# W2 in order of first appearance, W1 by id for 40 batches, row tables by three engines: an adapter layer with a language index

## The chip, the cores and the metric

The kernel runs on one core of a Trainium2 chip. The metric is the device time of one run in microseconds; the medians of several runs are compared. A core has five engines with queues of their own: TensorE (PE), VectorE (DVE), ScalarE (ACT), GpSimd (POOL) and SyncE (SP, here a queue of DMAs alone). Each works through its instructions in order and waits for the others by semaphores. The DMAs of all queues share 16 DMA engines.

## The reference

x holds 128 batches of 128 positions with 512 features, float32. Each batch has a language id (0 to 8 in the data, ten languages in the tables), and everything but x is looked up by it:

```
h       = relu(x @ W1[id] + b1[id])            # W1[id] 512x128
adapted = h @ W2[id] + b2[id]                  # W2[id] 128x512
y       = x + adapted
normed  = (y - mean(y)) * rsqrt(var(y) + 1e-5) # over the 512 features
out     = x + normed * gamma[id] + beta[id]
```

x and the output are 33.6 MB each; W1 and W2 are 2.6 MB each for all ten languages, 256 KB for one.

## The kernel before

One batch is one tile, 128 positions on the partitions. Loads of x come in groups of four batches (1 MB, four buffers), output leaves in pairs (512 KB, five buffers), both on SP's queue in program order. The order of each engine's instructions is written out by hand: `keep` ties an instruction to the one before it on its engine.

Per batch b the engines do this:

- PE: `transpose_x` (four products with the identity into the one buffer of pool `p_x`), `down` (W1, four chunks), `up` (W2, looked up in the table `w2` by a register holding the id).
- ACT: `copy_xT` (transposed x to SBUF), `relu`, `stage_w1` (copies W1 of this batch's id from a table in SBUF to `w1s`), `square` (sum of squares), and small work for mean and deviation.
- POOL: `add_b2` (r = x + b2[id], for most batches) and `add_beta` (o = x + beta[id]).
- DVE: `vector_b2` (the b2 add, for the batches that POOL leaves out), `residual` (adds r or x and sums), `scale` (minus mean, times gamma), `finish` (times rstd, plus o). `store` follows on SP.

The b2 row of a batch is added by one of three: POOL, DVE (`b2_by_vector`) or PE (`b2_by_matmul`, one more product that picks the row from `parts`).

The tables beta_b, gamma_b and b2_b hold each language's row on all 128 partitions (gamma's times -0.5). Before the loop, DVE splits the 30 rows into three bfloat16 parts, PE spreads each row with one product (`spread`, into the five buffers of pool `p_y` that `up` uses too), and DVE (17) and ACT (13) copy them out. These 30 turns stand between the first transposes, downs and relus.

W1 comes in two ways. Batches 0 to 8 (`FIRST`) read it from DRAM by their id, with the feature order "(p k)", so that x is transposed with a stride as well. From batch 9 `stage_w1` copies it from SBUF: up to batch 20 from `w1e` (same order, loaded in two DMAs), then from `w1` (four DMAs of 640 KB with rows of 512 bytes). W2 is loaded in id order, three languages and then seven.

In the loop, turn i transposes x of batch i, does down(i-1) and up(i-2), and the DVE work of batch b = i-3. A table indexed by a register is waited for as a whole, as far as the register's declared largest value reaches.

Of the kernel before, what the change touches and what calls it, by code (L numbers as in the profile page):

```python
# [16 lines left out]
P = 128  # L17
G = 4
EPS = 1e-5
FIRST = 9  # L20
EARLY = 21
LATE = 12
# [4 lines left out]
def cond_resid_kernel(ctx: ExitStack, tc: tile.TileContext, x, itok, W1, b1, W2, b2, gamma, beta, out):  # L27
# [31 lines left out]
    wp = ctx.enter_context(tc.tile_pool(name="wp", bufs=5))  # L59
# [18 lines left out]
    ids = const.tile([1, B], I32, name="ids")  # L78
# [3 lines left out]
    w1e = const.tile([P, L, KC, A], FP, name="w1e")  # L82
    w2 = const.tile([P, L * H], FP, name="w2")
    x_0 = xp.tile([P, G, H], FP, tag="x", name="x_0")
    xs[0] = x_0
# [5 lines left out]
    keep(nc.sync.dma_start(out=ids, in_=itok.rearrange("(o b) -> o b", o=1)))  # L91
    keep(nc.scalar.dma_start(out=rows[0:L, :], in_=beta))
    keep(nc.sync.dma_start(out=rows[L : 2 * L, :], in_=gamma))
    keep(nc.scalar.dma_start(out=rows[2 * L : 3 * L, :], in_=b2))
    load_part(0, 2)
# [4 lines left out]
    keep(nc.scalar.activation(warm, warm, AF.Abs_reciprocal_sqrt))  # L100
    def load_w1(k):
        keep(
            nc.sync.dma_start(out=w1[:, :, k, :], in_=W1[:, k * P : (k + 1) * P, :].rearrange("l p a -> p l a"))
        )

    ident = const.tile([P, P], FP, name="ident")
    make_identity(nc, ident)
    eps = const.tile([P, 1], FP, name="eps")
    nc.gpsimd.memset(eps, EPS)
    ones = const.tile([P, P], BF, name="ones")  # L110
    nc.gpsimd.memset(ones, 1.0)
# [3 lines left out]
    R = 3 * L  # L115
# [6 lines left out]
    keep(nc.vector.tensor_scalar(pick[:, L : 2 * L], pick[:, L : 2 * L], -0.5, None, ALU.mult))  # L122
# [4 lines left out]
    wrap = const.tile([1, B], I32, name="wrap")  # L127
    keep(nc.vector.tensor_scalar(wrap, ids, 0, L, ALU.is_lt, ALU.mult))
    lang = const.tile([1, B], I32, name="lang")
    keep(nc.vector.tensor_tensor(lang, ids, wrap, ALU.add))  # L130
    keep(nc.vector.tensor_scalar(lang, lang, 0, L - 1, ALU.max, ALU.min))

    def lid(b, engine):
        g = b // G
        if (g, engine) not in lids:
            loads, vals = nc.values_load_multi_w_load_instructions(  # L136
                lang[0:1, g * G : (g + 1) * G],
                engines=[engine],
                min_val=0,
                max_val=L - 1,  # L140
                skip_runtime_bounds_check_because="clamped on the chip to 0..L-1 above",
            )
            for ins in loads:
                keep(ins)
            lids[g, engine] = vals
        return lids[g, engine][b % G]

# [3 lines left out]
    def load_first(b):  # L151
        w1s[b] = wp.tile([P, KC, A], FP, tag="w1s", name=f"w1s_{b}")
        src = W1[bass.ds(lid(b, ET.SP), 1)].rearrange("o (p k) a -> p (o k a)", k=KC)
        keep(nc.sync.dma_start(out=w1s[b].rearrange("p k a -> p (k a)"), in_=src))

    def load_w2(lo, hi):
        dst = w2[:, lo * H : hi * H].rearrange("p (l h) -> p l h", l=hi - lo)
        keep(nc.sync.dma_start(out=dst, in_=W2[lo:hi].rearrange("l a h -> a l h")))

    def load_early(lo, hi):  # L160
        dst = w1e[:, lo:hi].rearrange("p l k a -> p l (k a)")
        keep(nc.sync.dma_start(out=dst, in_=W1[lo:hi].rearrange("l (p k) a -> p l (k a)", k=KC)))

    load_w2(0, 3)
    load_first(0)
    load_first(1)
    load_part(2, G)
    load_first(2)
    load_first(3)
    load_w2(3, L)  # L170
    xs[1] = xp.tile([P, G, H], FP, tag="x", name="x_1")
    for b in (G, G + 2):
        load_part(b, b + 2)
        load_first(b)
        load_first(b + 1)
    xs[2] = xp.tile([P, G, H], FP, tag="x", name="x_2")
    load_part(2 * G, 2 * G + 2)
    load_early(0, 5)
    load_first(2 * G)
    load_early(5, L)  # L180
    load_part(2 * G + 2, 3 * G)

    left = rp.tile([P, H], FP, tag="r", name="left")
    keep(nc.vector.tensor_copy(parts[0:R, :], rows[0:R, :]))
    keep(nc.vector.tensor_tensor(left[32 : 32 + R, :], rows[0:R, :], parts[0:R, :], ALU.subtract))
    keep(nc.vector.tensor_copy(parts[32 : 32 + R, :], left[32 : 32 + R, :]))
    keep(nc.vector.tensor_tensor(left[64 : 64 + R, :], left[32 : 32 + R, :], parts[32 : 32 + R, :], ALU.subtract))
    keep(nc.vector.tensor_copy(parts[64 : 64 + R, :], left[64 : 64 + R, :]))
# [7 lines left out]


    beta_b = const.tile([P, L * H], FP, name="beta_b")
    gamma_b = const.tile([P, L * H], FP, name="gamma_b")
    b2_b = const.tile([P, L * H], FP, name="b2_b")  # L200

    def spread(r, copier):
        t = (beta_b, gamma_b, b2_b)[r // L]
        row = p_y.tile([P, H], FP, tag="y", name=f"row_{r}")
        pick_r = pick[:, r : r + 1].to_broadcast([96, P])
        keep(nc.tensor.matmul(row, lhsT=pick_r, rhs=parts[:96, :], start=True, stop=True))
        dst = t[:, r % L * H : (r % L + 1) * H]
        if copier is nc.scalar:
            keep(nc.scalar.copy(dst, row))
        else:  # L210
            keep(nc.vector.tensor_copy(dst, row))  # L211
# [5 lines left out]
    def b2_by_matmul(b):  # L217
        return b in (5, B - 1)

    def b2_by_vector(b):  # L220
        return b < 4 or 8 <= b < B - 8 and (b % 4 == 1 if b < 24 else b % 16 in (1, 6, 11) or b % 32 == 30)

    def stage_w1(b):
        w1s[b] = wp.tile([P, KC, A], FP, tag="w1s", name=f"w1s_{b}")
        src = (w1e if b < EARLY else w1).rearrange("p l k a -> p (l k a)")[:, bass.ds(lid(b, ET.Activation) * (KC * A), KC * A)]
        keep(nc.scalar.copy(w1s[b].rearrange("p k a -> p (k a)"), src))  # L226

    def transpose_x(b):
        pxs[b] = p_x.tile([P, KC, P], FP, tag="xT", name=f"pxT_{b}")
        for k in range(KC):  # L230
            if b < EARLY:
# [36 lines left out]
    def up(b):  # L268
        v = lid(b, ET.PE)
        ys[b] = p_y.tile([P, H], FP, tag="y", name=f"py_{b}")  # L270
        m = b2_by_matmul(b)
        if m:
            pick_b = pick[:, bass.ds(v + 2 * L, 1)].to_broadcast([96, P])
# [216 lines left out]
    spin(9, H)  # L490
    spin(1, H // 2)

    def spread_turn(lo, hi):
        for r in range(lo, hi):
            spread(r, nc.scalar if r % 7 in (1, 3, 5) else nc.vector)
# [4 lines left out]

    x_turn(0)
    transpose_b1()
    spread_turn(0, 4)
    x_turn(1)
    spread_turn(4, 11)
    down(0)
    relu(0)
    spread_turn(11, 15)
    down(1)
    relu(1)  # L510
    x_turn(2)
    spread_turn(15, 19)
    x_turn(3)
    down(2)
    relu(2)
    spread_turn(19, 24)
    down(3)
    relu(3)
    spread_turn(24, R)
    up(0)  # L520
    up(1)

    for i in range(3, B + U):
# [3 lines left out]
        if i == 5:  # L527
            load_x(3)
        if i in (8, 10, 12, 14):
            load_w1((i - 8) // 2)  # L530
        if i == 4:
            up(2)
        if i == 5:
            up(3)
        if i > 3 and on(i):
            transpose_x(i)
# [3 lines left out]
        if i > 4 and on(i - 1):  # L540
            down(i - 1)
        if i > 3 and on(i):
            copy_xT(i)
# [3 lines left out]
        if i > 4 and on(i - 1):  # L547
            relu(i - 1)
        if i + 1 >= LATE and on(i + 1):
            stage_w1(i + 1)  # L550
        if i > 5 and on(i - U):
# [41 lines left out]
        if FIRST <= i + 1 < LATE:  # L593
            stage_w1(i + 1)
# [41 lines left out]
```

## Time and profile before

| what | value |
|---|---|
| median of 3 runs | 308.49 us (308.26 to 308.88) |
| span of the profiled execution | 306.5 us |
| median less span | 2.0 us |
| PE, DVE, ACT, POOL busy | 294.6, 295.9, 282.3, 283.9 us |
| DMA moved | 77.85 MB, 254 GB/s on average |
| granted TensorE clock | 0.989 |

The profile is one execution; its own time is the span, from the first to the last instruction, and the sums of the prediction are made against it. A line of the timeline has start and duration in us, the engine, the source line, the operation with the tile written and read, the shape and the count, and in brackets the idle time before it with what ended it. A line of the waits has who waited, for whom, and total us, times and longest us. A duration of POOL overlaps that of its neighbour, so that its pitch is read from starts. PEld and PEldq are PE's weight loads and their queue; a q behind an engine's name is its instruction queue.

### The profile page before, as it was taken

To read this page: it belongs to the slowest core of one execution; us is meant where nothing else is said; L and a number is where in the kernel's file an instruction comes from. 1 tells how busy PE (TensorE), PEld (TensorE's weight loads), DVE (VectorE), ACT (ScalarE), POOL (GpSimd) and SP (SyncE) were. 2 spreads that over 40 slices of the span, in tenths; PEclk is the share of its full clock that TensorE was granted. 3 is DMA by queue.
4 is the path that set the end of the run, shared out by engine and by line. 5 is a ranking of instruction groups with operands and counts; after the bars stand their busy time and mean duration, and the time that the engine had idled before them with its cause. 6 is when DMAs were issued, how large, how long until landed. Compare 5 with 4: busy or idle time off the path is not lost. (4 is left out here: it accounts for less than half of the span.)

```text
span 306.5 us, 6981 instructions
## 1 busy us (share of the span) xinstructions
PE 294.6 (96%) x1835; PEld 220.0 (72%) x1835; DVE 295.9 (97%) x771; ACT 282.3 (92%) x777; POOL 283.9 (93%) x238
## 2 busy tenths in 40 slices
PE   8999999999999999999999999999999999999960
PEld 3748787777777777777777777777777777777730
DVE  6889999999999999999999999999999999999985
ACT  3858999999999999999999999999999999999981
POOL 1349899999999999999999999999999999999994
PEclk9999999999999999999999999999999999999995
DMA  6999999976678766766777666767776666773324
GB/s 231 379 390 388 373 371 354 387 231 240 221 255 276 250 202 241 226 257 219 259 276 243 213 209 238 265 224 260 275 238 206 226 231 242 246 266 137 135 109 171
DMA packets 43769, 77.85 MB, mean 254 GB/s; under 512 B 1961, under 2 KB 7348, under 8 KB 43730
## 3 DMA queue, kind: packets, MB, share of 16 engines
q1 hardware_dynamic: 43382, 76.84, 72.1%
q10 hardware_dynamic: 348, 0.57, 0.5%
q8 instruction: 15, 0.25, 0.3%
q14 instruction: 24, 0.20, 0.2%
HBM read 43.85 MB, written 33.55 MB: 253 GB/s over the span
## 5 line engine op out<-in xcount | busy, mean ns | idle before, releaser
L252 POOL TENSOR_TENSOR o<-x,beta_b 128x512 f32<-128x512 f32 x128 | 173.9, 1395 | 10.2 <-DVE beta_b L211 9.5
L245 POOL TENSOR_TENSOR r<-x,b_b 128x512 f32<-128x512 f32 x97 | 135.7, 1399 | 7.3 <-DVE b_b L211 6.2
L258 PE MATMUL ph<-xT,w1s 128*128 128x128 f32 x1024 | 135.4, 275 | 0.0
L275 PE MATMUL py<-w,hT 128*128 x256 | 131.2, 595 | 0.5 <-DVE b_b L211 0.5
L258 PEld LDWEIGHTS ph<-xT,w1s 128*128 128x128 f32 x1024 | 124.9, 192 | 1.0 <-ACT hT L266 0.5
L235 PEld LDWEIGHTS pxT<-ident,x 128*128 128x128 f32 x512 | 66.6, 151 | 65.3 <-issue 49.2
L358 DVE SCALAR_TENSOR_TENSOR py<-py,nmean,gamma_b 128x512 f32<-128x512 f32 x126 | 95.0, 754 | 0.9 <-ACT sq L399 0.8
L367 DVE SCALAR_TENSOR_TENSOR o<-py,rstd,o 128x512 f32<-128x512 f32 x122 | 91.2, 748 | 0.0
L315 ACT ACTIVATE sq<-py,sum 128x512 f32<-128x512 f32 x124 | 85.9, 693 | 2.8 <-DVE py L292 2.5
L235 PE MATMUL pxT<-ident,x 128*128 128x128 f32 x512 | 78.2, 276 | 0.0
L239 ACT COPY xT<-pxT 128x512 f32<-128x512 f32 x128 | 74.7, 584 | 3.5 <-PE pxT L235 3.5
L292 DVE SCALAR_TENSOR_TENSOR py<-py,r 128x512 f32<-128x512 f32 x97 | 67.0, 691 | 0.2
L226 ACT COPY w1s<-w 128x512 f32 x107 | 65.5, 612 | 0.0
L266 ACT ACTIVATE hT<-ph,b1T 128x128 f32<-128x128 f32 x128 | 46.9, 366 | 7.9 <-PE ph L258 2.6
L275 PEld LDWEIGHTS py<-w,hT 128*128 128x128 f32 x256 | 39.1, 192 | 2.9 <-issue 1.0
L315 ACT ACTIVATION_READ_ACCUMULATOR sq<-py,sum 128x1 f32 x124 | 25.0, 202 | 0.0
L292 DVE SCALAR_TENSOR_TENSOR py<-py,x 128x512 f32<-128x512 f32 x31 | 21.7, 699 | 0.4
L285 DVE TENSOR_TENSOR py<-py,b_b 128x512 f32<-128x512 f32 x29 | 20.2, 695 | 0.7 <-PE py L275 0.6
L325 ACT ACTIVATE root<-ssq,eps 128x2 f32<-128x2 f32 x62 | 16.4, 265 | 0.0
L292 DVE DVE_READ_ACCUMULATOR py<-py,r 128x1 f32 x97 | 13.7, 141 | 0.0
L306 ACT ACTIVATE nmean<-sum 128x2 f32<-128x2 f32 x62 | 12.3, 198 | 0.0
L329 DVE SCALAR_TENSOR_TENSOR part<-ssq,root 128x2 f32<-128x2 f32 x62 | 9.3, 151 | 0.2 <-ACT root L325 0.2
(55 smaller groups left out, 90.4 us busy)
## 6 DMA issues: line engine op xcount, KB each, us to landing
out_dram<-o SPq DMA_DIRECT2D x61, 512.0 KB, 3.4
x<-in_x_dram SPq DMA_DIRECT2D x29, 1024.0 KB, 6.2
x<-in_x_dram SPq DMA_DIRECT2D x6, 512.0 KB, 8.8
w1e<-in_L_cond_W_dram SPq DMA_DIRECT2D x2, 1280.0 KB, 12.3
w<-in_L_cond_W_dram SPq DMA_DIRECT2D x4, 640.0 KB, 8.1
w1s<-in_L_cond_W_dram SPq DMA_DIRECT2D x9, 256.0 KB, 8.4
w<-in_L_cond_W_dram SPq DMA_DIRECT2D x1, 1792.0 KB, 10.3
w<-in_L_cond_W_dram SPq DMA_DIRECT2D x1, 768.0 KB, 5.4
```

The source lines that it names most:

```text
L226: keep(nc.scalar.copy(w1s[b].rearrange("p k a -> p (k a)"), src))
L235: keep(nc.tensor.transpose(pxs[b][:, k, :], cols, ident))
L239: keep(nc.scalar.copy(xT[b], pxs.pop(b)))
L245: keep(nc.gpsimd.tensor_tensor(rs[b], xb(b), b2_b[:, bass.ds(v * H, H)], ALU.add))
L252: keep(nc.gpsimd.tensor_tensor(os[g][:, j, :], xb(b), beta_b[:, bass.ds(v * H, H)], ALU.add))
L258: nc.tensor.matmul(phs[b], lhsT=w1s[b][:, k, :], rhs=xT[b][:, k, :], start=(k == 0), stop=(k == KC - 1))
L266: keep(nc.scalar.activation(hT[b], phs.pop(b), AF.Relu, bias=b1T[:, bass.ds(lid(b, ET.Activation), 1)]))
L275: keep(nc.tensor.matmul(ys[b], lhsT=hT[b], rhs=w2[:, bass.ds(v * H, H)], start=not m, stop=True))
L292: nc.vector.scalar_tensor_tensor(ys[b], ys[b], 1.0, r, ALU.mult, ALU.add, accum_out=col(sums, b))
L315: nc.scalar.activation(sq, ys[b], AF.Square, bias=col(sums, b), scale=-float(H), accum_out=col(ssqs, b))
L358: nc.vector.scalar_tensor_tensor(ys[b], ys[b], col(nmeans, b), gamma_b[:, bass.ds(v * H, H)], ALU.add, ALU.mult)
L367: nc.vector.scalar_tensor_tensor(o, ys.pop(b), rstds[g][:, j : j + 1], o, ALU.mult, ALU.add)
```

## The change

- The ids are read onto ten partitions. VectorE finds the place of each language's first batch, one product with PE and a comparison give its rank, and two more products give `slots`: which language has each rank, and the rank of each batch's language. `load_slot(j)` loads the W2 of the language of rank j into slot j; `up(b)` takes the slot, and for b under 10 the slot is declared to be at most b, so that up(b) waits for slots 0 to b alone.
- W1 is read by id for batches 0 to 39 (`BY_ID`) into seven buffers (`RING`, before five); the table `w1e` and its 12 staged batches are gone, and `stage_w1` begins at batch 40. `ahead` strings W1, W2 and x loads together; the four `w1` loads stand at turns 16, 21, 26 and 31, before at 8, 10, 12 and 14.
- beta's rows: loaded at partitions 0, 32, 64 and 96, spread by ten VectorE shuffles of 128x512. b2's: loaded as one flat row on partition 0, spread by two GpSimd broadcasts of 2,560 columns each. gamma's ten rows stay with PE and ACT, five before up(0) and five in turns 3 to 5. The bfloat16 parts are taken by reading the upper halves of the float32 words.
- Batches 0 to 3 get b2 from PE (before from VectorE), batch 5 from GpSimd (before from PE).
- Six warming products stand at the start, before nine and a half; batches 0 to 2 (before 0 to 3) are transposed before the loop.

```diff
-FIRST = 9
-EARLY = 21
-LATE = 12
+BY_ID = 40
+RING = 7
...
+    lang = const.tile([L, B + 1], I32, name="lang")
+    keep(nc.sync.dma_start(out=lang[:, 0:B], in_=itok.rearrange("(o b) -> o b", o=1).to_broadcast([L, B])))
+    beta_rows = rp.tile([P, H], FP, tag="r", name="beta_rows")
+    nc.gpsimd.memset(beta_rows, 0.0)
+    for q in range(2):
+        keep(nc.scalar.dma_start(out=beta_rows[32 * q : 32 * q + L, :], in_=beta))
+    load_part(0, 1)
+    keep(nc.scalar.dma_start(out=rows[0:L, :], in_=gamma))
+    for q in range(2, 4):
+        keep(nc.scalar.dma_start(out=beta_rows[32 * q : 32 * q + L, :], in_=beta))
+    load_part(1, 2)
+    keep(nc.scalar.dma_start(out=rows[L : 2 * L, :], in_=b2))
+    load_part(2, 4)
+    keep(nc.scalar.dma_start(out=b2_b[0:1, :], in_=b2.rearrange("(o l) h -> o (l h)", o=1)))
     keep(nc.scalar.dma_start(out=b1r, in_=b1))
...
+    keep(nc.vector.scalar_tensor_tensor(seen, lang, own, weight, ALU.is_equal, ALU.mult))
+    keep(nc.vector.tensor_reduce(first, seen, mybir.AxisListType.X, ALU.max))
...
+    def rank_languages():
+        order = p_s.tile([P, H], FP, tag="s", name="order")
+        keep(nc.tensor.matmul(order[:L, 0:L], lhsT=first.to_broadcast([L, L]), rhs=ident[:L, :L], start=True, stop=True))
+        keep(nc.vector.tensor_tensor(rows[32 : 32 + R, :], rows[0:R, :], upper(rows, 0), ALU.subtract))
+        keep(nc.vector.tensor_scalar(above, order[:L, 0:L], first, None, ALU.is_gt, ALU.add, accum_out=rank))
+        keep(nc.vector.tensor_scalar(own_of, lang[:, 0:B], own, None, ALU.is_equal))
+        keep(nc.vector.tensor_scalar(place, count[:, 0:L], rank, None, ALU.is_equal))
+        keep(nc.vector.tensor_tensor(parts[64 : 64 + R, :], rows[32 : 32 + R, :], upper(rows, 32), ALU.subtract))
+        keep(nc.scalar.copy(parts[0:R, :], upper(rows, 0)))
+        keep(nc.scalar.copy(parts[32 : 32 + R, :], upper(rows, 32)))
+        return order
+
+    def place_languages(order):
+        keep(nc.tensor.matmul(order[:1, L : 2 * L], lhsT=own, rhs=place, start=True, stop=True))
+        keep(nc.tensor.matmul(order[:1, 2 * L : 2 * L + B], lhsT=rank, rhs=own_of, start=True, stop=True))
+        keep(nc.vector.tensor_copy(slots, order[:1, L : 2 * L + B]))
...
-    def load_first(b):
+    def load_by_id(b):
...
-    def load_w2(lo, hi):
-    def load_early(lo, hi):
+    def load_slot(j):
+        if j == 0:
+            v = lid(0, ET.SP)
+        else:
+            if not perm:
+                perm.extend(values(slots[0:1, 1:L], ET.SP, L - 1))
+            v = perm[j - 1]
+        src = W2[bass.ds(v, 1)].rearrange("o a h -> a (o h)")
+        keep(nc.sync.dma_start(out=w2[:, j * H : (j + 1) * H], in_=src))
...
-    def spread(r, copier):
+    def spread_gamma(lo, hi):
+        for r in range(lo, hi):
+            row = p_y.tile([P, H], FP, tag="y", name=f"row_{r}")
+            pick_r = pick[:, r : r + 1].to_broadcast([96, P])
+            keep(nc.tensor.matmul(row, lhsT=pick_r, rhs=parts[:96, :], start=True, stop=True))
+            keep(nc.scalar.copy(gamma_b[:, r * H : (r + 1) * H], row))
+
+    def spread_beta(lo, hi):
+        for r in range(lo, hi):
+            keep(nc.vector.stream_shuffle(beta_b[:, r * H : (r + 1) * H], beta_rows, [r] * 32))
+
+    def spread_b2(lo, hi):
+        cols = slice(lo * H, hi * H)
+        keep(nc.gpsimd.partition_broadcast(b2_b[:, cols], b2_b[0:1, cols]))
...
     def b2_by_matmul(b):
-        return b in (5, B - 1)
+        return b < 4 or b == B - 1
...
     def up(b):
-        v = lid(b, ET.PE)
+        v = slot(b)
...
-    spin(9, H)
-    spin(1, H // 2)
+    spin(6, H)
+    order = rank_languages()
...
+    def ahead(n):
+        if n == 3:
+            load_slot(1)
+            load_part(4, 6)
+        elif n == 5:
+            load_part(6, 8)
+        elif n == 7:
+            load_part(8, 10)
+        elif n == 9:
+            load_part(10, 12)
+        load_by_id(n)
+        if 3 < n < L + 2:
+            load_slot(n - 2)
+
+    spread_b2(0, L // 2)
+    spread_b2(L // 2, L)
     x_turn(0)
     transpose_b1()
-    spread_turn(0, 4)
+    place_languages(order)
     x_turn(1)
-    spread_turn(4, 11)
+    spread_gamma(0, 2)
+    spread_beta(0, 3)
     down(0)
     relu(0)
+    spread_gamma(2, 4)
+    spread_beta(3, 6)
+    x_turn(2)
+    for n in range(3, RING + 1):
+        ahead(n)
     down(1)
     relu(1)
...
+    spread_gamma(4, 5)
+    spread_beta(6, 10)
     up(0)
...
-        if i in (8, 10, 12, 14):
-            load_w1((i - 8) // 2)
+        if i in (16, 21, 26, 31):
+            load_w1((i - 16) // 5)
...
+        if i + RING - 2 < BY_ID:
+            ahead(i + RING - 2)
+        if i < 6:
+            spread_gamma(2 * i - 1, min(2 * i + 1, L))
...
-        if i + 1 >= LATE and on(i + 1):
+        if BY_ID <= i + 1 and on(i + 1):
             stage_w1(i + 1)
```

## The prediction

> **What bounds the kernel now.** I read the page's busy shares first, then the waits, then the timelines of PE and POOL from end to end, and last the DMA by stretches.
>
> ```profile
> PE 294.6 (96%) x1835; PEld 220.0 (72%) x1835; DVE 295.9 (97%) x771; ACT 282.3 (92%) x777; POOL 283.9 (93%) x238
> ```
>
> Four engines are over 90% busy, so no share names the bound; the waits do. All long ones of the engines lie in the first 20 us:
>
> ```profile
> POOL o L252 <- DVE beta_b L211: 9.5, 1, 9.5
> POOL r L245 <- DVE b_b L211: 6.2, 1, 6.2
> POOL r L245 <- DMA x<-in_x_dram: 1.1, 1, 1.1
> ```
>
> POOL waits for the row tables beta_b and b2_b, then once for x, and never again. Its timeline (start, us, line, count):
>
> ```profile
> 10.98 2.50 POOL L252 TENSOR_TENSOR o<-x,beta_b 128x512 f32<-128x512 f32 x2 [9.53 <-DVE beta_b L211]
> 19.67 1.27 POOL L245 TENSOR_TENSOR r<-x,b_b 128x512 f32<-128x512 f32 x1 [6.19 <-DVE b_b L211]
> ...
> 296.34 1.45 POOL L415 TENSOR_TENSOR n<-n,gamma_b 128x512 f32<-128x512 f32 x1
> ```
>
> From 19.67 to 296.34 it does 126 of the 128 beta adds and 97 b2 adds: (276.67 - 1.14 of wait) / 223 = 1.235 us each. PE:
>
> ```profile
> 18.94 2.81 PE L275 MATMUL py<-w,hT 128*128 x6 [0.46 <-DVE b_b L211]
> ...
> 26.92 0.63 PE L235 MATMUL pxT<-ident,x 128*128 128x128 f32 x4
> 29.36 0.63 PE L235 MATMUL pxT<-ident,x 128*128 128x128 f32 x4
> 31.58 0.63 PE L235 MATMUL pxT<-ident,x 128*128 128x128 f32 x4
> ...
> 290.88 0.60 PE L235 MATMUL pxT<-ident,x 128*128 128x128 f32 x4
> ```
>
> Batch 9 is transposed at 31.58, batch 127 at 290.88: 2.197 us a batch for 118 batches, back to back (transposes 0.43, down 0.90, up 0.86). So PE and POOL both run without a gap from about 20 us to about 296, and then comes a tail of 10 us. The end is the start of the steady stretch plus a fixed amount of work, on either engine: only the first 20 us can shorten. DVE has room once it starts: in its timeline two batches without a b2 add take 4.07 us (149.83 to 153.90).
>
> ```profile
> 28.00:32.00 4.00, 4.00 (x25) 3.02 (x25) 4.00 (x12) 3.12 (x10) 4.00 (x4) 1.00 1.05 382
> 44.00:48.00 4.00, 4.00 (x26) 3.05 (x26) 4.00 (x11) 3.86 (x13) 4.00 (x4) 1.00 1.08 344
> 52.00:56.00 4.00, 4.00 (x26) 3.06 (x26) 4.00 (x12) 3.86 (x12) 3.57 (x3) 1.00 1.08 397
> ```
>
> The last two columns are DMA share and GB/s: full at 380 to 390 until 62 us, and 344 to 373 (mean 360) from 36 to 52, where w1's 512-byte rows are read. After 64 us it is 240.
>
> **Start, part by part.** Only sums that reach POOL or PE count.
>
> POOL's first work grows by the memset of beta_rows. Memsets of 128x1 and 128x128 take 98 and 204 ns, so 128x512 is about 0.5 us. `ident`, with an iota ahead of it, comes 0.65 later. DVE's clamp of the ids moves from 2.80 to 3.45, and so does the first W1 load of SP, from 3.55 to 4.2. ACT's DMA queue holds seven small loads for two and waits for that memset: issues of about 0.33 us from 1.4 on, b2's rows at 3.35, the flat b2 row at 3.7, then the table load (1.28), ACT free at 5.95. Small loads landed 1.7 us after issue (b2's rows: 1.41, used at 3.1), so rows are there at 5.05 and the flat row at 5.7 (20 KB on one partition).
>
> DVE, in order: subtraction 5.05 (0.68), three small ops of 0.22 for rank and place, subtraction 0.68, b1T, slots: the ranking ends at 7.45. The two extra PE products (0.23 each, as b1p) lie in that time. Against before, DVE loses 17 copies (0.64 each, 10.9 us) and three casts, and gets ten shuffles. The trace has no shuffle: the cheapest row of 512 columns is the cast (0.42), the dearest DVE row 0.76; I take 0.62, the pitch of copies and residuals that also move one word per column. beta_b is complete at 7.45 + 6.2 = 13.65 (11.7 to 15.1).
>
> ACT and PE: two part copies (0.4) to 6.75, xT of batch 0 to 7.4, which frees the one transpose buffer. Then they alternate: row product 0.23, row copy 0.54, down 0.9, relu 0.35, up with its bias product 1.1. In turn: down(0) ends 9.2, relu(0) 9.9, xT(2) 11.55, up(0) starts 11.3 (18.94 before). Turns 3 to 5 still carry five gamma copies on ACT ahead of xT, 3.2 us a turn: batches 4, 5 and 6 are transposed at 15.65, 18.85 and 21.5, batch 7 at 23.8, where before has 26.92, and batch 9 at 28.2 for 31.58. So PE gains 3.4 us. The 20 row products that go (4.6 us) are more than that, since ACT is the slower partner here. The single register loads of the first ten batches (0.33 each on PE's queue) are hidden under 2.2 us of queued products a batch.
>
> POOL: the b2 broadcast writes 5,120 columns. Bounds from rows: the memset's slope (0.83 ns a column) gives 4.3 us, the two-input add (2.41) 12.35; nearest is the affine select, one tensor in and one out, (292 - 98)/127 = 1.5 ns, 7.8 us. From 5.7 it ends at 13.5 (10.0 to 18.05). The built program also selects another POOL code library ahead of the broadcasts and the first one again behind them. Before has one such selection ahead of the affine select, which started at 1.16 with POOL's memset just over: zero cost there. I take zero, and keep the dear end as a rival. So POOL's first add waits for both tables and starts at 14.2, half a microsecond after beta_b. From there it has 226 adds (128 and 98: batch 5 comes to POOL, batches 0 to 3 were never on it): 226 x 1.235 = 279.1, and L415 starts at 293.3 for 296.34. POOL gains 3.0 us. Break-even is a first add at 17.2.
>
> DVE: four b2 adds less (0.7 each), start 13.65 for 20.13: it gains more than both and follows. ACT loses the w1s copies of batches 9 to 39 (31 x 0.51), off the path: it has had slack.
>
> **DMA.** W1 by id for 40 batches is 10.5 MB, with w2 and w1 15.7 against 10.2 before: 5.5 MB more in the full stretch. A unit of 256 KB takes 0.68 us at 388 GB/s. A by-id batch moves three (x, W1, output): 2.03 us, under PE's 2.20. SP's queue now holds W2's slot 1, and all behind it, until the ranking is read, about 8.3. Down to batch 12's W1 there are 39 units: landed at 3.0 + 0.8 lost in that wait + 39 x 0.68 = 30.3, wanted at 28.2 + 3 x 2.2 + 2.65 = 37.4: 7 us in hand. 28 batches add 4.8; the four w1 loads (2.62 MB at 360 and the slowing of what runs beside them) take 8. So 3.8 us stay at batch 40: hidden, narrowly. SP issues W1 in line behind output stores that wait for DVE, so a load goes out some 11 to 14 us ahead of its product; loads of this kind took
>
> ```profile
> DMA to landing us min/median/max: 4.5/8.4/10.4
> ```
>
> from issue to landing. That is the cover, and 1 to 3 us of PE time are lost where it fails.
>
> **Sum.** PE -3.4, POOL -3.0; the later decides: -3.0. The span 306.5 becomes 303.5; the runs' median lies 2.0 above the span, so 305.5.
>
> **Rivals.**
> 1. *The library change is a code load* (ends slower). POOL stands at it twice, at 2.45 and behind the broadcasts, and every add queues behind. If each takes what the shortest W1 load took to land, 4.5 us, the first add is at 2.45 + 4.5 + 7.8 + 4.5 = 19.3, 2.1 us past break-even: 310.6; at the median 8.4 it is 27.1 and 318. It decides from 3.5 us each. For it: two changes that before has not. Against: the one selection there cost nothing, though that may be since the library was already in. I take 312 for it.
>
> The Trainium skill (GPSIMD Engine Reference, section 2.1, Instruction dispatch) says that the first call into a freshly loaded kernel pays a code load of about 6 us that no instruction in the profile shows. By it the sum would be a first add at 22.3 us and a run of 313.5, an estimate from that page; no run here shows it so far, and the zero gap ahead of the affine select speaks against it only if that library too was fresh.
>
> 2. *DMA runs dry between batches 16 and 40.* If the mixed rate stays at 360 rather than 388, a by-id batch takes 2.18 us, nothing is regained, and the w1 loads leave the queue about 1 us short, with the late issue 1 to 3: 306.5 to 308.5. For it: 344 in one stretch; against: 397 with stores running.
> 3. *The broadcast costs what an add costs a column*, 12.35 us: first add 18.05, 0.85 later than break-even: 309.3. For it: POOL's only wide operation here has that price; against: it reads two tensors.
>
> **Numbers.** Forecast 0.50 (own range 304.2 to 306.3, from beta_b at 13 to 15), rival 1 0.27, rival 2 0.15, rival 3 0.08. The range 304.2 to 312.3 leaves out the dear half of rival 1 and a little below. Less than 0.2% (0.6 us) can't be told from no change. Faster: 0.50 and most of rival 2, 0.62. Same 0.05, from rivals 2 and 3. Slower 0.33.
>
> **What would show it.** Right: POOL's first add near 14 and no POOL wait later, up(0) near 11.3, batch 9 transposed near 28, batch 127 near 287.5, DMA at 380 to 100 us with no PE wait for w1s. Wrong: a gap on POOL of several us on either side of the broadcasts (rival 1), PE waiting for DMA w1s around 50 to 95 us (rival 2), or shuffles over 0.97 us each, which would put beta_b past 17.2.

## The result and the profile after

The changed kernel takes 315.81 us (median, 315.61 to 317.11) where the kernel before takes 308.48 (308.26 to 308.88): ratio 1.0245, 95% interval 1.0226 to 1.0265. It is slower by 7.3 us, and the prediction's range, 304.2 to 312.3, does not hold it. The profiled span is 313.9 us for 306.5.

The page's line of busy shares, changed kernel:

```profile
PE 293.9 (94%) x1820; PEld 219.5 (70%) x1820; DVE 290.9 (93%) x774; ACT 269.1 (86%) x745; POOL 291.4 (93%) x246
```

PE's and DVE's shares fell a little and ACT's by six points; no new engine is full. Of the waits that are new (us in total, times, longest), four bear on what follows:

```profile
POOL o L303 <- DVE py L343: 10.2, 1, 10.2
POOL b_b L262 <- DVE parts L177: 7.4, 1, 7.4
...
PE b1p L246 <- DMA b1r<-in_L_cond_b_dram: 4.8, 1, 4.8
...
PE pxT L286 <- DMA x<-in_x_dram: 1.7, 3, 0.7
```

POOL stands 7.4 us ahead of b2's broadcasts and 10.2 behind them. POOL's timeline (start, us, line, idle before) shows what that does:

```profile
10.10 5.48 POOL L262 PARTITION_BROADCAST b_b<-b_b  x2 [7.41 <-DVE parts L177]
25.75 2.50 POOL L303 TENSOR_TENSOR o<-x,beta_b 128x512 f32<-128x512 f32 x2 [10.18 <-DVE py L343]
...
304.38 1.27 POOL L466 TENSOR_TENSOR n<-n,gamma_b 128x512 f32<-128x512 f32 x1
```

The releasers named are not the cause. The broadcasts end at 15.58, the last of beta's shuffles at 17.92 in VectorE's timeline, and the first add comes 7.8 us after that. The timeline shows nothing in between. Asked for by source line, the profile does: POOL's queue holds an instruction that changes POOL's code library (count, duration in ns, first and last start in us), here in the kernel before and then twice in the changed kernel:

```profile
masks.py:199 POOLq MODIFY_POOL_CONFIG  x2: 11/11/11, 1.1 to 1.1; - x2
L262 POOLq MODIFY_POOL_CONFIG  x2: 1/1/1, 2.7 to 2.7; - x2
L303 POOLq MODIFY_POOL_CONFIG  x2: 127/127/127, 15.5 to 15.5; - x2
```

The one in the kernel before cost nothing (its affine select starts at 1.16), nor did a first one at 1.7 in the changed kernel. Behind the two shown for the changed kernel, POOL stands until 10.10 and until 25.75. From 25.75 the 226 adds run without a gap, 1.233 us each, and the first multiply of the tail stands at 304.38 for 296.34: 8.0 later.

PE's timeline, batches 0, 1 and 9 and the last:

```profile
4.68 0.75 PE L286 MATMUL pxT<-ident,x 128*128 128x128 f32 x4
10.26 0.27 PE L246 MATMUL b1p<-ident,b1r 10*128 10x10 f32 x1 [4.83 <-DMA b1r<-in_L_cond_b_dram]
...
12.80 1.80 PE L309 MATMUL ph<-xT,w1s 128*128 128x128 f32 x8
...
16.68 1.02 PE L326 MATMUL py<-w,hT 128*128 128x512 f32 x2
...
34.32 0.63 PE L286 MATMUL pxT<-ident,x 128*128 128x128 f32 x4
...
297.73 0.60 PE L286 MATMUL pxT<-ident,x 128*128 128x128 f32 x4
```

PE does nothing between 5.4 and 10.3 us, since the transpose of b1 waits for b1's small load. Batch 9 is transposed at 34.32 for 31.58, batch 127 at 297.73 for 290.88. So PE is 2.7 us late after the start and 6.9 at the end. Of the other 4.1, 3.8 are lost between batches 10 and 40, which take 70.0 us for 66.2.

DMA by stretches (the last two columns are its share and GB/s), kernel before:

```profile
0.00:16.00 16.00, 14.76 (x75) 8.89 (x76) 11.57 (x26) 9.32 (x18) 3.37 (x10) 1.00 0.84 309
16.00:64.00 48.00, 47.55 (x292) 36.08 (x291) 46.94 (x118) 42.69 (x119) 42.54 (x35) 1.00 1.05 375
64.00:104.00 40.00, 40.00 (x255) 30.21 (x255) 39.88 (x105) 39.22 (x110) 40.00 (x33) 1.00 0.69 228
```

and the changed kernel:

```profile
0.00:16.00 16.00, 9.35 (x43) 6.12 (x44) 9.01 (x34) 6.12 (x12) 7.33 (x15) 0.79 0.49 164
16.00:64.00 48.00, 46.73 (x282) 34.69 (x281) 39.71 (x105) 36.02 (x101) 38.25 (x32) 1.00 1.04 381
64.00:104.00 40.00, 38.62 (x239) 29.41 (x238) 38.14 (x99) 29.82 (x85) 40.00 (x34) 1.00 1.06 392
```

Multiplied out, DMA has moved 4.9 MB at 16 us before and 2.6 after: 2.3 MB behind, 5.9 us at 390 GB/s. From there it is full until 104 us, where before it was full only until 62.

The issues of ScalarE's and SyncE's queues show where the first 16 us went:

```profile
4.20 0.29 ACTq L105 DMA_DIRECT2D rows<-in_L_cond_b_dram  x1
4.53 0.26 ACTq L107 DMA_DIRECT2D b_b<-in_L_cond_b_dram  x1
6.92 0.29 ACTq L108 DMA_DIRECT2D b1r<-in_L_cond_b_dram  x1
7.23 1.28 ACT L112 ACT_TABLE_LOAD   x1 [7.23 <-DMA rows<-in_L_cond_b_dram]
```

```profile
6.68 0.85 SPq L223 DMA_DIRECT2D w1s<-in_L_cond_W_dram  x2
13.51 0.33 SPq L235 DMA_DIRECT2D w<-in_L_cond_W_dram  x1
```

In the built program the loads of both queues use eight completion semaphores in turn, and a load is not issued before the one eight earlier has landed. So b1's load waits from 4.8 to 6.92, the table load behind it to 7.23, the ranking ends at 11.42 with PE's b1 wait inside it, and SyncE, which reads the ranked slots ahead of everything else, issues nothing for 6 us. The last 1.9 of these are the read itself, nine values at once (duration in ns, start in us):

```profile
L188 SPq TENSOR_LOAD <-slots x1: 1875/1875/1875, 11.4 to 11.4; - x1
```

SyncE's reads of a single id in the kernel before took 304 to 491 ns.

Two bounds, then, are each some 7 us late by themselves: POOL (first add 25.75) and PE (batch 127), whose loss behind the start falls into the stretch in which DMA is now full. The experiments take them apart.

### The profile page after: what moved, and what is told of

Its sections match the earlier page's. It is cut to its first block, busy times and chain, and to the rows that moved or that the text cites. A ratio compares the mean times of both kernels' runs of the same rounds, so it can differ in the third digit from the quotient of the medians.

```text
span 313.9 us, 7122 instructions
## 1 busy us (share of the span) xinstructions
PE 293.9 (94%) x1820; PEld 219.5 (70%) x1820; DVE 290.9 (93%) x774; ACT 269.1 (86%) x745; POOL 291.4 (93%) x246
## 4 chain that ended last, share of the span: by engine, by line
PE 41%; POOL 30%; DMA 13%; issue 10%; POOLq 2%; DVE 1%; ACT 1%; ACTq 1%; SPq 0%; DVEq 0%
POOL o L303 18%; PE ph L309 16%; PE py L326 14%; POOL r L296 11%; PE pxT L286 9%; DMA x<-in_x_dram 7%; DMA w1s<-in_L_cond_W_dram 2%; DMA out_dram<-o 2%; DMA beta_rows<-in_L_cond_beta_dram 1%; POOLq L188 1%; DMA b1r<-in_L_cond_b_dram 1%; POOL n L466 1%; PE row L253 1%; POOLq L296 1%; POOL o L468 1%
## 5 line engine op out<-in xcount | busy, mean ns | idle before, releaser
L303 POOL TENSOR_TENSOR o<-x,beta_b 128x512 f32<-128x512 f32 x128 | 161.4, 1269 | 10.2 <-DVE py L343 10.2
L326 PE MATMUL py<-w,hT 128*128 (+1 forms) x256 | 131.3, 594 | 0.0
L296 POOL TENSOR_TENSOR r<-x,b_b 128x512 f32<-128x512 f32 x98 | 124.1, 1266 | 0.0
L286 PEld LDWEIGHTS pxT<-ident,x 128*128 128x128 f32 x512 | 68.1, 161 | 71.2 <-issue 44.5
L286 PE MATMUL pxT<-ident,x 128*128 128x128 f32 x512 | 79.8, 279 | 2.7 <-DMA x<-in_x_dram 1.7
L343 DVE SCALAR_TENSOR_TENSOR py<-py,r 128x512 f32<-128x512 f32 x98 | 67.7, 691 | 2.1 <-PE py L326 0.8
L277 ACT COPY w1s<-w 128x512 f32 x88 | 53.9, 613 | 0.0
L336 DVE TENSOR_TENSOR py<-py,b_b 128x512 f32<-128x512 f32 x25 | 17.3, 692 | 0.9 <-PE py L326 0.7
L262 POOL PARTITION_BROADCAST b_b<-b_b x2 | 5.5, 2800 | 7.4 <-DVE parts L177 7.4
```

The lines of the kernel that those rows point to most:

```text
L286: keep(nc.tensor.transpose(pxs[b][:, k, :], cols, ident))
L296: keep(nc.gpsimd.tensor_tensor(rs[b], xb(b), b2_b[:, bass.ds(v * H, H)], ALU.add))
L303: keep(nc.gpsimd.tensor_tensor(os[g][:, j, :], xb(b), beta_b[:, bass.ds(v * H, H)], ALU.add))
L326: keep(nc.tensor.matmul(ys[b], lhsT=hT[b], rhs=w2[:, bass.ds(v * H, H)], start=not m, stop=True))
L343: nc.vector.scalar_tensor_tensor(ys[b], ys[b], 1.0, r, ALU.mult, ALU.add, accum_out=col(sums, b))
```

## Experiments

Times are medians; the kernel before, run beside them, is 308.46 to 308.77. "First add" is POOL's first beta add, "b10", "b40" and so on the start of that batch's transposes, read off PE's timeline (before: 33.8 and 100.0).

### Each bound taken away: a1, c1, c2

a1 puts a memset where the two broadcasts stood, so POOL changes no library for them (b2's table is zeros).

```diff
-        keep(nc.gpsimd.partition_broadcast(b2_b[:, cols], b2_b[0:1, cols]))
+        keep(nc.gpsimd.memset(b2_b[:, cols], 0.0))
```

> The changed kernel with a GpSimd memset of b2's table in place of the two broadcasts, so b2 is left out for the batches that read the table. No second code library is needed. Theory S (the change of library delays POOL's adds): POOL's first add starts within 0.3 us of the last shuffle, near 18.0 instead of 25.75, and the time falls from 315.8 to about 311, where the late PE start (batch 9 transposed at 34.3, 2.7 us later than before) becomes the bound. Rival (POOL waited for DVE or a load): the first add stays near 25 and the time at 315 to 316.

315.47 us (1.0225, 1.0187 to 1.0263). POOL's timeline of a1:

```profile
7.54 4.49 POOL L262 MEMSET b_b<- 128x2560 f32 x2 [5.15 <-DMA b_b<-in_L_cond_b_dram]
17.54 2.50 POOL L303 TENSOR_TENSOR o<-x,beta_b 128x512 f32<-128x512 f32 x2 [5.51 <-DVE beta_b L258]
```

The first add comes 8.2 us earlier, and the gap goes with the broadcasts: the library changes are the cause of POOL's two waits. They do not weigh alike. The memset here waits until 7.54 for b2's flat row, so ahead of the broadcasts the change adds about 2.6 us to a wait that was there anyway; the change back counts in full. But the time stays, where 311 was expected. b10 is 37.0, b40 107.5: 70.5 us, as in the changed kernel. Another bound stands at the same place.

c1 lightens DMA instead: 20 batches by id rather than 40. c2 does both.

```diff
-BY_ID = 40
+BY_ID = 20
-        if i in (16, 21, 26, 31):
-            load_w1((i - 16) // 5)
+        if i in (5, 8, 11, 14):
+            load_w1((i - 5) // 3)
```

> The changed kernel with W1 by id for 20 batches instead of 40 (w1's four loads at turns 5, 8, 11, 14): 5.2 MB less DMA before batch 40, the library changes kept. Two bounds theory (the library changes and the DMA of the by-id batches each put the end at the same place): POOL's first add stays near 25.7 and its adds run on without a gap, so the time stays within 1.5 us of 315.8, although DMA is no longer full to 104 us. If DMA alone is the bound: 311 to 312. If the library alone were the bound, the same as by both; the next run tells that apart.

> 20 batches by id and the memset in place of the broadcasts (b2 left out where the table is read): both suspected bounds are taken away at once. Two bounds theory: batch 10 transposed near 37 as in the changed kernel, batch 40 30 x 2.2 = 66 us later (70 with 40 by id), near 103, and the time 311 to 312.5. The memset alone gave 315.5; if the library were the only bound besides the start, this would be 315.5 again.

c1: 315.73 us (1.025, 1.0218 to 1.0282), first add 25.57 and no POOL wait after it; batches 10 to 40 take 66.9 us. c2: 313.04 us (1.0139, 1.0117 to 1.0161). Neither bound alone is worth anything that can be measured; both together give 2.8 us. Two bounds are shown, and that 4.3 us are lost to something else (c2 is 0.5 over its expectation): in c2 b10 stands at 37.8 and the first add at 18.32, both later than before, and DMA has 158 GB/s over the first 16 us.

### The price of a library change: b1

The kernel before with one broadcast of eight scratch columns behind POOL's constants, and nothing else.

```diff
+    probe = const.tile([P, 8], FP, name="probe")
+    nc.gpsimd.memset(probe, 0.0)
+    keep(nc.gpsimd.partition_broadcast(probe, probe[0:1, :]))
```

> The kernel before with a GpSimd broadcast of eight columns of a scratch tile after POOL's constants, so that the code library changes there and back, and nothing else. Theory S: the first add, at 10.98 before, starts at 17 to 20, and the time rises by 0 to 3 us, since POOL had until 17.2. If a change of library costs nothing: first add at 11 and the same time.

309.59 us (1.0032, 1.0021 to 1.0044). POOL's timeline:

```profile
1.65 0.10 POOL L113 MEMSET probe<- 128x8 f32 x1
10.83 0.28 POOL L114 PARTITION_BROADCAST probe<-probe  x1 [9.08 <-DVE beta_b L214]
21.64 2.50 POOL L255 TENSOR_TENSOR o<-x,beta_b 128x512 f32<-128x512 f32 x2 [10.53 <-DVE py L288]
```

9.1 us into the other library and 10.5 back, for a broadcast of 0.28; in the changed kernel 7.4 and 10.2. The instruction that changes the library stands at 1.7 and at 11.0. Against the before's first add at 10.98 the delay is 10.7 us, but most of it falls into POOL's old wait for b2's table: the first b2 add starts at 24.10 for 19.67. Of these 4.4 us POOL saves 1.8 of waits that it had later, its tail starts 2.5 later, and the run loses 1.0. So the place of a library change counts as much as its size.

### The small loads: a2 and a3

ScalarE's queue gets gamma's, b2's and b1's rows first, then the table load, and beta's four loads last; a3 has a1's memset as well.

```diff
-    for q in range(2):
-        keep(nc.scalar.dma_start(out=beta_rows[32 * q : 32 * q + L, :], in_=beta))
     keep(nc.scalar.dma_start(out=rows[0:L, :], in_=gamma))
...
     keep(nc.scalar.dma_start(out=rows[L : 2 * L, :], in_=b2))
     keep(nc.scalar.dma_start(out=b1r, in_=b1))
...
     keep(nc.scalar.activation(warm, warm, AF.Abs_reciprocal_sqrt))
+    keep(nc.scalar.dma_start(out=b2_b[0:1, :], in_=b2.rearrange("(o l) h -> o (l h)", o=1)))
+    for q in range(4):
+        keep(nc.scalar.dma_start(out=beta_rows[32 * q : 32 * q + L, :], in_=beta))
```

> The changed kernel with ACT's queue put in another order: gamma's, b2's and b1's rows first, then the table load, then the flat b2 row and beta's four loads. Theory Q (the small loads on ACT's queue held each other up, so that PE stood 4.8 us for b1's rows): PE has no such wait, up(0) starts near 12 instead of 16.5, beta_b is complete near 15 instead of 17.9. The library change stays, so by theory S POOL's first add is still at 22 to 25 and the time only falls to 312 to 315. If S were wrong, the time would fall to about 306 here. Rival to Q (b1's rows come late for DMA traffic, not for the queue's order): up(0) stays near 16.

> Both edits: memset in place of the broadcasts (b2 left out where the table is read) and ACT's queue in the other order. By S and Q together this is the start that the prediction drew: up(0) near 12, first add near 15, and 305 to 306.5. If loads by id limit the stretch to batch 40, 307 to 309 with PE waits for x or W1 between 50 and 100 us.

a2: 317.13 us (1.0279, 1.0262 to 1.0296). PE no longer waits for b1 and the first up product starts 1.5 us earlier, but beta's rows now come late, and POOL's first add (25.41) is set by the library as before: no gain, a miss. a3: 314.25 us (1.017, 1.0131 to 1.0209), 1.2 under a1 with intervals that overlap, for 305 to 306.5 expected. W2's slot 1 is issued at 8.81 for 13.51 and b10 is 35.8 (a1: 37.0), but batches 10 to 40 take 70.8 us, as in a1.

### A complete kernel with neither bound: f1, f1_id40

b2's rows are loaded by four small loads on SyncE's queue and spread by ten more shuffles, ScalarE's queue is sorted as in a2 with beta ahead of the table load, batches 4 and 5 get b2 on PE, and 20 batches are by id; f1_id40 has 40.

```diff
-        keep(nc.gpsimd.partition_broadcast(b2_b[:, cols], b2_b[0:1, cols]))
+        for r in range(lo, hi):
+            keep(nc.vector.stream_shuffle(b2_b[:, r * H : (r + 1) * H], b2_rows, [r] * 32))
...
-        return b < 4 or b == B - 1
+        return b < 6 or b == B - 1
```

> A complete kernel: b2's rows by ten more VectorE shuffles (after residual 0 and 1), so no library change; the small loads in another order; b2 by PE for batches 0 to 5; 20 batches by id. The three losses found are gone: up(0) near 12.5, beta_b near 14, batch 10 near 32 to 33.5 (before 33.8), and 306 to 308.3. If shuffles hold up DVE's first residuals more than PE's five buffers cover, 309 to 310.

> The same complete kernel with 40 batches by id and w1's loads at turns 16, 21, 26 and 31 as in the change. DMA theory: batches 10 to 40 take 69 to 71 us again, and the time is 4 to 5 us above the one with 20 by id, 311 to 313. If by-id loads are hidden: equal within 0.7 us.

f1: 311.37 us (1.0098, 1.0074 to 1.0121). beta is complete at 13.9 and the first add at 13.99, where the prediction had 13.65 and 14.2; then POOL waits 4.9 us for b2's table:

```profile
23.81 1.27 POOL L296 TENSOR_TENSOR r<-x,b_b 128x512 f32<-128x512 f32 x1 [4.85 <-DVE b_b L262]
```

b10 is 35.2, where 32 to 33.5 was expected (and 306 to 308.3 us). f1_id40: 312.90 (1.015, 1.0126 to 1.0174), 10 to 40 in 68.9 us for f1's 66.3. The bytes cost 1.5 us here, not the 4 to 5 expected. And f1, without the library changes and with half of the loads by id, is still 2.6 us behind.

### An earlier start: g1, g2, g3

f1's first products are slow. g1 fills PE's idle 1.5 us ahead of them with three warming products; g2 takes ScalarE's copies (the two of the split rows, then gamma's) out of the chain from one transpose to the next, sets down(0) ahead of the first gamma rows and two of b2's shuffles ahead of residual 0; g3 does both.

```diff
     place_languages(order)
+    spin(3, H)
```

```diff
     x_turn(0)
+    copy_parts()
...
-        if i < 6:
-            spread_gamma(2 * i - 1, min(2 * i + 1, L))
         if on(i):
             copy_xT(i)
...
             relu(i - 1)
+        if i < 6:
+            spread_gamma(2 * i - 1, min(2 * i + 1, L))
```

> f1 (b2 by shuffles, 20 batches by id) with three more warming products on TensorE after the ranking's last product, at 6.4 us, where PE stood idle until 7.9. Nothing else moves. In f1 the first down product took 1.91 us and the second 1.46, for 1.06 in the kernel before, and each transpose group and row pair about twice its later time, though the profile's clock column says 1.00. Theory W (PE slows down after standing idle, and this is what f1 lost): from 7.9 on, the transposes of batch 1 take 0.63, the first down 1.06, and batch 10 is transposed about 1.5 us earlier than in f1 (33.7 for 35.2), the time is about 310 (f1 311.4). Theory O (PE's pace does not matter there, because the turns wait for ScalarE's copies in a chain): the products get shorter, but batch 10 stays at 35 and the time within 0.3 us of f1.

> f1 with the order of ScalarE's work at the start changed, and no work added: the copy of batch 0's transposed x stands ahead of the two copies that split the rows, the first down product ahead of the first gamma rows, the gamma rows of turns 3 to 5 behind the turn's xT copy and relu instead of ahead, and two of b2's ten shuffles ahead of residual 0, so that b2's table is done sooner. Theory O (the chain transposes, down, rows, gamma copies, xT copy, next transposes sets turns 3 to 5): those turns take 3.2 us for 3.5, the first down starts near 8 for 9.7, batch 10 is transposed at 33 for 35.2 and the time is 309 to 309.5. Theory W (PE's slow start): batch 10 at 34.5 or later and the time over 310.5.

> Both edits of the two kernels named before on f1: the warming products and ScalarE's order. If both causes hold, and since neither POOL (first add at 14, its wait for b2's table 3 to 4 us) nor DMA binds there, batch 10 is transposed at about 32, 1.8 us ahead of the kernel before (33.8), and the time is 306.5 to 307.5, under the kernel before. If POOL's wait for b2's table takes over, 308 to 309. If only one of them counts, its own result.

311.65 (1.0112, 1.0096 to 1.0128), 311.39 (1.009, 1.0073 to 1.0106) and 311.59 us (1.0107, 1.0093 to 1.0121): no change from f1, where g3 was to come under the kernel before. The means worked. The first down product of f1 and of g1:

```profile
9.69 1.91 PE L309 MATMUL ph<-xT,w1s 128*128 128x128 f32 x8
```

```profile
9.76 1.18 PE L309 MATMUL ph<-xT,w1s 128*128 128x128 f32 x8
```

b10 moves from 35.2 to 33.3, 33.4 and 32.0, as both theories hoped. But b30 is 79.4 in f1 and 80.0, 80.1 and 80.0 in these: all of it is lost again within 20 batches. PE's waits in g3:

```profile
37.20 1.10 PE L328 MATMUL py<-w,hT 128*128 x2 [1.33 <-DMA w<-in_L_cond_W_dram]
58.45 1.13 PE L311 MATMUL ph<-xT,w1s 128*128 128x128 f32 x8 [1.28 <-ACT w1s L279]
```

the first for a slot of W2, the second for a copy out of w1, started at 57.70, whose last load landed at 57.67. POOL waits 6.3 us in all for output stores. DMA is full at 390 GB/s from 16 to 64 us, after 214 over the first 16. Both theories asked about the engines, and what was late was DMA.

### DMA's first 16 us: h1, h2, h3

h1 is g3 with more loads ahead of SyncE's read of the ranked slots. h2 has 15 batches by id instead of 20 (w1 at turns 4, 6, 8, 10), h3 has 40.

```diff
     load_by_id(2)
-    for q in range(4):
-        keep(nc.sync.dma_start(out=b2_rows[32 * q : 32 * q + L, :], in_=b2))
+    load_part(4, 6)
+    load_by_id(3)
+    load_by_id(4)
...
             load_slot(1)
-            load_part(4, 6)
+        elif n == 4:
+            load_slot(2)
+            for q in range(4):
+                keep(nc.sync.dma_start(out=b2_rows[32 * q : 32 * q + L, :], in_=b2))
```

> g3 (b2 by shuffles, 20 batches by id, warm start, ScalarE's order) with SyncE's queue rearranged: x of batches 4 and 5 and W1 of batches 3 and 4 are issued before SyncE reads the ranked slots, and the four small loads of b2's rows come behind W2's slots 1 and 2. No bytes are added or taken away. In g3 the DMA engines moved 4 GB/s from 10 to 12 us and 199 to 227 on either side, about 3.5 us without work, and were full at 390 from 16 to 64; batch 30 was at 80.0 however early the start was. Theory D (DMA's idle stretch at the start is what g1 to g3 cannot get under): no stretch under 300 GB/s from 4 us on, batch 30 about 3 us earlier (77), POOL's waits for output stores gone, and the time 306.5 to 308.5. Theory P (the end is set by POOL's late first adds alone): batch 30 still at 79.5 to 80 and the time over 310.5.

> The same with W1 by id for 15 batches and w1's four loads at turns 4, 6, 8 and 10: 1.3 MB less, 3.4 us less of DMA time at 390 GB/s. Theory D: batch 30 at 75 to 76 if the start allows it and w1 lands in time for batch 15 (PE waits for w1s otherwise), time 305 to 307. Theory P: as the kernel named before, no change.

> The same with W1 by id for 40 batches, as the change has it, and w1's loads at turns 16, 21, 26 and 31. Theory D, first form (the 5.2 MB more cost their time, 13 us at 390 GB/s less what a by-id batch has in hand under PE's 2.20, 28 x 0.17, and less what waits at batch 10): 10 to 40 in 68 us or more, batch 40 at 102 or later, time 1 to 2 us over the kernel with 20. Second form (the bytes were hidden and only the idle stretch at the start took the reserve): 10 to 40 in 66.5 us or less and the same time as with 20.

h1: 310.76 us (1.0067, 1.0041 to 1.0092); b30 80.3. The edit did not do what it should: the idle stretch was broken up, not removed. DMA has 244 GB/s over the first 16 us and then 319 from 16 to 20, and at 64 us it has moved 22.1 MB, as in g3 (before 22.9, f1 22.5). Slot 1 now goes out at 12.34, and b2's rows land so late that VectorE waits 2.3 us for them. The slots have been ready since 6.77; the loads ahead wait for semaphores until 9.89, and SyncE's read of the slots then takes 1.88 us again (in f1 2.13, from 8.56). So the time, over 310.5, is the one named for theory P, but with the stretch still there it does not decide between the theories. h2: 315.11 us (1.0218, 1.0196 to 1.0239), because w1 is wanted before it has come; ScalarE's timeline:

```profile
49.58 0.62 ACT L280 COPY w1s<-w 128x512 f32 x1 [3.17 <-DMA w<-in_L_cond_W_dram]
```

and b20 falls to 62.2 for 57.0. h3: 313.96 us (1.0184, 1.0158 to 1.0211), 3.2 over h1, with 10 to 40 in 69.9 us: here the bytes do cost.

### One part alone in the kernel before: q1, p1

q1 reads W1 by id for 40 batches, without ranking and without the early copy w1e, in seven buffers. p1 takes beta's rows by shuffles, and gives the copies of gamma's rows to ScalarE.

```diff
-FIRST = 9
-EARLY = 21
-LATE = 12
+FIRST = 40
+EARLY = 40
+LATE = 40
...
-        if i in (8, 10, 12, 14):
-            load_w1((i - 8) // 2)
+        if i in (16, 21, 26, 31):
+            load_w1((i - 16) // 5)
```

```diff
     def spread(r, copier):
+        if r < L:
+            keep(nc.vector.stream_shuffle(beta_b[:, r * H : (r + 1) * H], beta_rows, [r] * 32))
+            return
```

> The kernel before with W1 by id for 40 batches alone: no ranking, W2 and w1 as before but w1's four loads at turns 16, 21, 26 and 31, no early copy of W1, seven W1 buffers. 5.2 MB more are read, and SyncE waits for nothing new at the start. The kernel before had moved 4.9 MB at 16 us and 32.1 at 104; the changed kernel 2.6 and 36.6. Theory I (the idle stretch at the start, 2.3 MB or 5.9 us at 390 GB/s, took the reserve; the bytes by themselves are hidden, as the prediction had it): batch 10 near 34, 10 to 40 in 66.2 to 67, time 308 to 309.3. Theory B (the bytes alone are too many): 10 to 40 in 68.5 us or more, batch 40 past 102.5, time 310 or more.

> The kernel before with beta's ten rows by VectorE shuffles alone, and the copies of gamma's rows given to ScalarE, of b2's to both. VectorE's row work at the start is then ten shuffles (6.4 us) and seven copies (4.5), 10.9 as before (17 copies), and PE has ten row products less (2.3 us). Theory S (VectorE's rows set POOL's first adds): no change, 308.2 to 309. If the row products on PE were the bound: batch 10 two us earlier (32) and 306.5. If the four small loads delay ScalarE's table load and the first xT copy: up to 1.3 us slower, 309.5.

q1: 310.19 us (1.006, 1.0038 to 1.0081). DMA by stretches:

```profile
0.00:16.00 16.00, 14.76 (x79) 9.19 (x80) 12.12 (x27) 9.77 (x19) 3.38 (x10) 1.00 0.86 312
16.00:64.00 48.00, 47.51 (x289) 36.01 (x288) 46.90 (x119) 36.97 (x104) 44.19 (x36) 1.00 1.03 365
64.00:104.00 40.00, 40.00 (x254) 31.36 (x253) 39.76 (x104) 32.78 (x93) 36.09 (x30) 1.00 1.05 378
```

b10 33.4, b40 100.0, b127 290.84: PE loses nothing, as theory I had it, though the time is the one of theory B. DMA is as full until 104 us as in the changed kernel, but has its 5.0 MB at 16 us. So 40 batches by id fit under PE where the start is that of the kernel before.

That the changed kernel lost this for want of the 2.3 MB is not shown, and the landings, read from the semaphore updates in the trace, speak against it. In the changed kernel W1 of batches 10 to 39 landed 3.9 to 8.6 us ahead of its product and the x groups of batches 12 to 43 6.1 to 10.0 us ahead of their transposes; in q1 it is 3.9 to 10.6 and 4.1 to 8.4. What PE loses in the changed kernel lies for the most part in four turns, those of batches 20, 28, 32 and 36, each the first of its x group and each ending while the next group's x is landing. In q1 the same batches are transposed 0.4 to 2.2 us before that landing begins, and without a wait. What holds PE in these turns stays open.

What q1 does lose is POOL's, 4.3 us of waits for output stores to leave their buffers, all between 59 and 98 us. Of the stores issued from 60 to 100 us, those whose landing the trace has took 7.5 to 9.2 us there, and 3.3 to 4.4 in the kernel before, where DMA was no longer full:

```profile
POOL o L245 <- DMA out_dram<-o: 4.3, 5, 1.2
```

and the multiply of the tail starts at 298.75 for 296.34. p1: 309.15 us (1.0036, 1.0011 to 1.0061), b10 33.9, the tail's multiply at 296.72: the shuffles by themselves gain nothing, because VectorE's row work stays about as long as it was and the four loads push it back (first b2 add at 19.95 for 19.67).

No version run here beats the kernel before.

## Why the prediction was wrong, step by step

- **The library change at zero: wrong, and the step that alone would have been enough.** The prediction took the change ahead of the affine select as the sample. That one did cost nothing, why is not shown (the prediction named a library that was in already); the two new ones took 7.4 and 10.2 us, twice or more the 3.5 at which rival 1 decided, and c1 stays at 315.73 with DMA relieved. By the prediction's own sum for POOL, a first add at 25.75 ends 226 x 1.235 later, at 304.9; measured 304.38. So the arithmetic of POOL held, and rival 1 was the case, at its dear end (27.1 and 318) rather than at the 312 taken for it. The Trainium skill (GPSIMD Engine Reference, section 2.1, Instruction dispatch) gives about 6 us for the first call into a freshly loaded kernel, unseen among the instructions: it pointed the right way. The runs show 7.4 to 9.1 on the way in, and that the way back to the first library costs as much again, 10.2 to 10.5; the load has no row of its own, only the instruction that orders it.
- **"0.8 lost in that wait" and "hidden, narrowly": wrong.** SyncE's wait for the ranking and its read of the slots (1.9 us, where the prediction had 0.85 between the end of the ranking and that of the read) left DMA 2.3 MB, 5.9 us, behind. That did not empty the reserve, since PE started 6.1 us later than forecast as well: W1 of batch 12 landed 7.0 us ahead of its product, the prediction's figure by two errors that cancel. PE lost 3.8 us between batches 10 and 40 all the same, and the loads by id are what it takes: with 20 of them c2 needs 66.4 us there, with 40 a1 needs 70.5. So a loss of the size of rival 2 was there, but not for a queue that ran dry of W1. What held is 0.67 us a unit for 0.68 (392 GB/s from 64 to 104 us) and, in q1, 40 batches by id hidden under PE.
- **The small loads: wrong.** Issues "of about 0.33 us from 1.4 on" hold up to 4.8, but the next waits for a semaphore. b2's rows were issued at 4.20 and landed at 7.27, 3.1 us for the 1.7 taken; b1's rows, for which the sum had no term, at 10.26. So the ranking ended at 11.42 and not 7.45, beta at 17.92 and not 13.65, and the first W2 product of batch 0 started at 16.68 and not 11.3.
- **PE gains 3.4, POOL 3.0: not had by any kernel.** f1's first add stood where the prediction put it, with no library change and the small loads in order, and it still lost 2.6 us: its b2 table and b10 were late. g1 to g3 then had b10 1.8 us ahead of the kernel before at best, and gave all of it back by b30. The prediction read "the end is the start of the steady stretch plus a fixed amount of work" from PE and POOL. It did weigh DMA, but by W1 alone and with 0.8 us for the wait: g3 has moved 3.4 MB at 16 us for 4.9, and PE waits for a slot of W2 and for w1.
- **Turns 3 to 5 at 3.2 us:** 3.4, 3.5 and 3.0. Small, and the kind of chain was right.
- **Right:** the memset (0.52 for 0.5), the shuffle's pitch (0.64 for 0.62), the broadcasts within their bounds (5.48 for 4.3 to 12.35; 7.8 taken, so rival 3 is out).

The signs named as "wrong" were the ones seen: gaps of several us on either side of the broadcasts, and PE waiting between 59 and 98 us (the profile puts it down to DMA's x, where W1 was named; by its landings that x was there).

What stays open, beside PE's four turns: the 2 to 3 us that f1 to h1 still lose. That they are DMA's late start is argued from the bytes moved by 64 us (22.1 to 22.5 MB for 22.9) and from b30 standing at 79.4 to 80.3 whatever b10 was. No run here had both the ranking and a full DMA from 4 us on, so it is not shown. POOL's own times divide the loss: the tail is as late as the first b2 add, less three adds that no longer stand behind it (3.7 us), plus what POOL waits more behind it, nearly all for output stores while DMA is full. In f1 that is 4.1 - 3.7 + 2.0, in g3 2.2 - 3.7 + 4.9, in h1 5.7 - 3.7 + 1.7, for tails 2.6, 3.6 and 3.9 us late. So in h1 the late b2 table weighs as much as the stores, and theory P is not ruled out.

## What to carry to other kernels

Two rivals are not alternatives: each may hold, and then the later of two equal bounds hides what the removal of either is worth, so take away both in one run before you judge one. When an order is worked out on the chip, count the wait for it, the read of it, and the bytes that the transfer queue does not move meanwhile; and read the reserve where the data are used, from landing to first use, before a lost byte is called the cause. An operation of a kind that the trace does not have is not free because its neighbour was: try it alone, at its smallest.

## What the runs showed of the hardware

- A change of POOL's code library took 7.4 to 9.1 us to the broadcast's library and 10.2 to 10.5 back, with nothing in the timeline but the gap, even around a broadcast of 0.28 us (b1). One change ahead of an affine select cost nothing (kernel before).
- The partition broadcast itself is cheap: 2.80 us for 128 x 2560 in f32, 1.1 ns a column, less than half of the two-input add's 2.41.
- SyncE's read of nine values from an SBUF tile into registers took 1.88 us (changed kernel, h1) and 2.13 (f1), that of one value 0.30 to 0.49 (kernel before).
- In the changed kernel and in f1, PE's early products took up to twice their later time until about 14 us: the first down 1.80 us in the first, where the granted clock column reads 0.50 from 8 to 12 us, but also 1.91 in f1, where that column reads 1.00; later ones took 1.06. With three products of filler ahead of them it took 1.18 (g1). The column alone does not show it.
